# Spectral norms moved from the kernel's start into its first attention phase, in a two-layer attention kernel on one NeuronCore

## The chip, the core and the metric

The kernel runs on one NeuronCore of a Trainium2 chip. The metric is device time in microseconds (us), the median of several runs. Engines are named as in the profile: PE is TensorE's matrix multiply and PEld its weight load, DVE is VectorE, ACT is ScalarE, POOL is GpSimd, and SP is SyncE, which here only issues DMAs. ACTq and SPq are the issuing queues of ACT and SP.

## The reference, cut to what matters

Two layers run on x of shape (8, 64, 64, 256), in float32. The first layer is windowed attention over horizontal strips (half of the channels) and vertical strips (the other half), with a depthwise 3x3 convolution added. The second is attention over all 4096 positions of an image, with three small projections f, g and h and one out, v. The weights of these four are divided by their spectral norm, estimated with one power step:

```python
def _sn_kernel(w, u):
    wr = w.reshape(-1, w.shape[-1])
    v = _l2n(u @ wr.T)
    u2 = _l2n(v @ wr)
    sigma = v @ wr @ u2.T
    return w / sigma[0, 0]
...
qkv = x @ w_qkv + b_qkv                 # first layer
q, k = jnp.split(qkv, 2, axis=-1); v = k
context = jnp.concatenate([ch, cv], axis=-1)      # attention in strips
context = hard_swish(context + bias_branch)       # plus the convolution
x1 = context @ w_out + b_out
...
f = x1 @ kf + bf;  g = x1 @ kg + bg;  h = x1 @ kh + bh   # second layer
beta = softmax(g f^T)
out = gamma * ((beta h) @ kv + bv) + x1
```

The norms depend on weights alone. They are small: three weights of 256x32 and one of 32x256.

## The kernel before, in words

**Units and steps.** For each of the 8 images there are 8 horizontal units, 8 vertical units and 2 global units. A horizontal or vertical unit has 4 steps, a global one 32. A step computes a block of scores on PE (L696 or L877, four strips of 32 rows into two of three PSUM pairs), takes the exponential on ACT (L494, two pieces of 128x1024), and, one step later, multiplies the weights with the values (L713 or L893). Unit h0 takes the steps 0 to 3, h1 4 to 7, h2 8 to 11, h3 12 to 15, h4 16 to 19, and so on.

**What fills the steps.** Between scores and weighted sums PE does other work: the projections of x (L261, `project`: 32 matmuls of 128x256 for one group of 128 channels of one block of 512 positions), the sums of the weights (L731), later the projections of the second layer (L800, L827) and the outputs. ACT also evicts projections (L568 `qh`, L583 `kh`, L571, L586, L587), copies sums and results (L514 `copy_sums`, L743 `release`), and starts each convolution with its first tap (L635). DVE does the other eight taps of a convolution (L639), adds weights (L722, L904), and turns tiles (L504 to L507, L649).

**One bank.** Projections, sums, `norms`, `combined_weights` and some others all use one PSUM tile with the tag `mm` (L291). It has one buffer, so each of them waits until the last one's result was copied out of it.

**The planner.** The order of every engine's instructions is fixed when the program is built. `Flow` (L76) keeps a clock for each engine, worked out from the prices in L51 to L55. Each piece of extra work is a `Task` with a due step, a step from which it is ready, the tasks it needs, and a chain of (engine, price) pairs. `Flow.step` (L207) writes the scores, then work that is due, then the weighted sums of the step before, then in `fill_pe` (L147) more work for PE: of the tasks that may begin, the one whose bank is already open, or else the one that is due first; of two with the same due step, the one added first. A task with `bank=True` may begin only when the planner's clock has passed `bank_free`. Then `fill_act` and `fill_dve` (L193) give those engines tasks until their clocks have caught up with PE's. Whatever a task's function issues goes to the engines' queues at that point, in program order on each engine.

**`combined_weights`** (L448) multiplies the normed weights of f, g and h by `w_out` once, so that the second layer's projections can read the first layer's context. It is a task with ready 16 and due 24; it runs at 136.54 us.

**The start.** Ahead of the planner's steps, the program loads the weights. On SP: `w_qkv` (L303), `b_qkv` (L305) and four copies of `wv`, one for each quarter of the partitions (L323); then the planner's first load of x (`load`, L551). On ACT: `wfgh` in three pieces (L308), `u_r`, `uv_r` and `gam` (L316), `w_out` (L328), `dw` (L330), `dw_bias` (L332), `b_out` (L334), `bfgh` (L336) and `bv` (L338). Then come the norms: products and sums on DVE (L350 to L367), three groups of matmuls with ones on PE (L370, L371), a copy of the result out of `mm` (L375), DVE again (L378 to L388), one Sqrt on ACT (L389), and the scaling of the weights (L390 to L396). `w_out` and `dw` are multiplied by 1/6 (L397, L398). The temporary tiles lie in a pool, `prep`, that is closed at the end (L399), and its space is used again.

**The range of sums.** Each unit writes the reciprocals of its sums into `recs`, a tile of 128x18x16 per image. At an image's end `note` (L545) takes the elementwise maximum and minimum of `recs` and two tiles `seen`, also 128x18x16. After the last image `limits` (L411) reduces these to one value a row, compares them with bounds, and writes a flag; if a bound is passed, an exact but slower loop runs afterwards (L1334). It doesn't run here.

Of the kernel before, what the change touches and what calls it, by code (L numbers as in the profile page):

```python
# [23 lines left out]
D = 32  # L24
NQ = P // D
L2_EPS = 1e-12
# [4 lines left out]
def quad(r):  # L31
    return slice(r * D, (r + 1) * D)
# [20 lines left out]
ADD, NORM, SWISH, TAP, TAPS = 2.36, 2.5, 0.75, 0.75, 1.28  # L53
# [211 lines left out]
def tile_attention_blocks(  # L265
# [31 lines left out]
    ones = const.tile([P, P], F32, name="ones")  # L297
# [8 lines left out]
    raw = const.tile([P, 2, 3, D], F32, name="raw")  # L306
# [1 line left out]
        nc.scalar.dma_start(out=raw[:, :, z, :], in_=wfgh[z].rearrange("(k p) m -> p k m", p=P))  # L308


    prep_ctx = ExitStack()
    prep = prep_ctx.enter_context(tc.tile_pool(name="prep", bufs=1))

    def rows(ap, n, name):
        t = prep.tile([P, n], F32, name=name)
        nc.scalar.dma_start(out=t, in_=ap.to_broadcast([P, n]))  # L316
        return t

    u_r = rows(ufgh.rearrange("z o d -> o (z d)"), 3 * D, "u_r")

    wv_raw = prep.tile([P, C], F32, name="wv_raw")
    for r in range(NQ):
        nc.sync.dma_start(out=wv_raw[quad(r), :], in_=wv)  # L323
    uv_r = rows(uv, C, "uv_r")
    gam = rows(gamma, 1, "gam")

    wout_sb = const.tile([P, 2, C], F32, name="wout_sb")
    nc.scalar.dma_start(out=wout_sb, in_=w_out.rearrange("(k p) m -> p k m", p=P))  # L328
    dw_sb = const.tile([P, 2, 9], F32, name="dw_sb")
# [3 lines left out]
    bout_c = const.tile([P, 2], F32, name="bout_c")  # L333
# [3 lines left out]
    bv_c = prep.tile([P, 2], F32, name="bv_c")  # L337
    nc.scalar.dma_start(out=bv_c, in_=bv)  # L338

    wcomb = const.tile([P, 2, 3 * D], F32, name="wcomb")  # L340
    bcomb = const.tile([P, 2], F32, name="bcomb")
    wv_sb = const.tile([P, C], F32, name="wv_sb")
    bias_o = const.tile([P, 2], F32, name="bias_o")


    NF = 3 * D + 3
    flat = raw.rearrange("p k z d -> p k (z d)")
    ext = prep.tile([P, 2, NF], F32, name="ext")
    a_f = prep.tile([P, 2, 3], F32, name="a_f")
    nc.vector.tensor_mul(  # L350
        ext[:, :, : 3 * D], flat, u_r.unsqueeze(1).to_broadcast([P, 2, 3 * D])
    )
    nc.vector.tensor_reduce(
        a_f, ext[:, :, : 3 * D].rearrange("p k (z d) -> p k z d", d=D), AX.X, ALU.add
    )
    for k in range(2):
        nc.vector.tensor_mul(
            ext[:, k, : 3 * D].rearrange("p (z d) -> p z d", d=D), raw[:, k],
            a_f[:, k, :].unsqueeze(2).to_broadcast([P, 3, D]),
        )  # L360
    nc.vector.tensor_mul(ext[:, :, 3 * D :], a_f, a_f)
    ext_v = prep.tile([P, C + 1], F32, name="ext_v")
    a_v = prep.tile([P, 1], F32, name="a_v")
    nc.vector.tensor_mul(ext_v[:, :C], wv_raw, uv_r)
    nc.vector.tensor_reduce(a_v, ext_v[:, :C], AX.X, ALU.add)
    nc.vector.tensor_scalar_mul(ext_v[:, :C], wv_raw, a_v)
    nc.vector.tensor_mul(ext_v[:, C:], a_v, a_v)  # L367
    pb = mm_tile("norms")
    for k in range(2):
        nc.tensor.matmul(pb[:, :NF], lhsT=ones, rhs=ext[:, k, :], start=(k == 0), stop=(k == 1))  # L370
    nc.tensor.matmul(  # L371
        pb[:, NF : NF + C + 1], lhsT=ones[:D, :], rhs=ext_v[:D, :], start=True, stop=True
    )
    sums = prep.tile([P, NF + C + 1], F32, name="sums")
    nc.vector.tensor_copy(sums, pb[:, : NF + C + 1])  # L375

    a2, b2, inv = (prep.tile([P, 4], F32, name=n) for n in ("a2", "b2", "inv"))
    nc.vector.tensor_copy(a2[:, :3], sums[:, 3 * D : NF])  # L378
    nc.vector.tensor_copy(a2[:, 3:], sums[:, NF + C :])
    nc.vector.tensor_mul(sums, sums, sums)  # L380
    nc.vector.tensor_reduce(
        b2[:, :3], sums[:, : 3 * D].rearrange("p (z d) -> p z d", d=D), AX.X, ALU.add
    )
    nc.vector.tensor_reduce(b2[:, 3:], sums[:, NF : NF + C], AX.X, ALU.add)
    nc.vector.tensor_scalar_max(a2, a2, L2_EPS)
    nc.vector.reciprocal(a2, a2)
    nc.vector.tensor_mul(b2, b2, a2)
    nc.vector.tensor_scalar_max(inv, b2, L2_EPS)  # L388
    nc.scalar.activation(inv, inv, AF.Sqrt)  # L389
    nc.vector.reciprocal(b2, b2)  # L390
    nc.vector.tensor_mul(inv, inv, b2)
    for k in range(2):
        nc.vector.tensor_mul(raw[:, k], raw[:, k], inv[:, :3].unsqueeze(2).to_broadcast([P, 3, D]))

    nc.vector.tensor_scalar(wv_sb, wv_raw, inv[:, 3:], gam, ALU.mult, ALU.mult)
    nc.vector.scalar_tensor_tensor(bias_o, bv_c, gam, bout_c, ALU.mult, ALU.add)  # L396
    nc.vector.tensor_scalar_mul(wout_sb, wout_sb, 1.0 / 6.0)  # L397
    nc.vector.tensor_scalar_mul(dw_sb, dw_sb, 1.0 / 6.0)  # L398
    prep_ctx.close()  # L399


    seen = [const.tile([P, 2 * NB + 2, TB // D], F32, name=f"seen{i}") for i in range(2)]
    for t in seen:
        nc.gpsimd.memset(t, 1.0)

    check = ctx.enter_context(tc.tile_pool(name="check", bufs=1))
    lim = check.tile([P, 2], F32, name="lim")
# [14 lines left out]
    def attention(images, load_x, out_rows, exact):  # L422
# [113 lines left out]
        def image(b):  # L536
            hv, qh, kh, kn, xt, vs, part = {}, {}, {}, {}, {}, {}, {}

            @cache
            def recs():  # L540
                return work.tile(
                    [P, 2 * NB + 2, TB // D], F32, tag="recs", name=f"recs_{b}", bufs=out_bufs
                )

            def note():  # L545
                for t, op in zip(seen, (ALU.max, ALU.min)):
                    nc.vector.tensor_tensor(t, t, recs(), op)

            def load(i):
                xt[i] = xpool.tile([P, 2, TB], F32, tag="x", name=f"x_{b}_{i}")  # L550
# [297 lines left out]
            def global_unit(z):  # L848
# [149 lines left out]
        units, t = [], 0  # L998
# [118 lines left out]
        def inside_due(i, far):  # L1117

            n = i + min(i, INSIDE) + far
            return DUE["spread0"] + (DUE["spread1"] - DUE["spread0"]) * n // (NB + INSIDE)  # L1120

        for n, im in enumerate(ims):
# [4 lines left out]
            for i in range(NB):  # L1127
# [32 lines left out]
                for half in range(2):  # L1160
# [50 lines left out]
            for kind, k in (("f", 0), ("f", 1), ("h", 0), ("f", 2), ("f", 3), ("h", 1)):  # L1211
# [10 lines left out]
                else:  # L1222
# [9 lines left out]
                        bank=True,  # L1232
# [156 lines left out]
```

## Time and profile before

| what | value |
| --- | --- |
| time, median of 3 runs | 3414.65 us (3414.16 to 3418.29) |
| the profiled execution's own time | 3416.28 us |
| its span, first to last instruction | 3414.5 us |
| mean granted PE clock | 0.996 of full |
| PE, DVE, ACT, POOL busy | 3331.6, 2860.6, 2668.8, 63.5 us |
| first projection of x on PE | at 12.94 us |
| scores of step 0, step 8, step 16, step 24 | at 21.84, 59.07, 97.40, 135.47 us |

In lines of the order of time and of the groups, the columns are: start in us, length in us, engine, line of the code, operation, output<-input, shape, count, and in brackets the idle time of that engine just before and what ended it. In the view of waits, the columns are: who waited, for whom, us in total, times, and the longest. In the chain of waits: start, length, what. A busy time of PE is modelled, and neighbouring groups of matmuls overlap by a little.

Some durations of the start, which no other place of the kernel shows: DVE's first part of the norms takes 1.29 us (from L350 to the end of L361) and 1.33 us (L364 to the end of L367); the matmuls take 1.15 and 1.22 us; from the copy L375 to the end of L388 pass 2.45 us; Sqrt takes 0.21 us; the rest, L390 to L395, about 1.2 us. From issue to landing, `w_qkv` takes 4.2 us and the first block of x 4.5 us (each 512 KB); the median of all blocks of x is 3.7 us. The small loads take between 2.9 and 4.3 us.

### The profile page before, as it was taken

How to read it: one execution, taken by the hardware profiler on the slowest of the kernel's cores; microseconds unless marked ns; L12 is line 12 of the kernel's file. 1: busy time of each engine (PE TensorE's matmuls, PEld its weight loads, DVE VectorE, ACT ScalarE, POOL GpSimd, SP SyncE). 2: the span in 40 equal slices, each digit the busy share in tenths (PEclk: the TensorE clock that was granted, in tenths of full speed). 3: DMA queues.
4: the chain of work that ended last, by engine and by line, in shares of the span. 5: the costliest groups of instructions: out<-in, count | busy, mean ns of one | idle time of the engine just before them, and what ended most of it. 6: DMA issues, size and time to landing. Idle time of an engine off the chain costs nothing.

```text
span 3414.5 us, 78286 instructions
## 1 busy us (share of the span) xinstructions
PE 3331.6 (98%) x33780; PEld 1126.4 (33%) x33780; DVE 2860.6 (84%) x2340; ACT 2668.8 (78%) x3235; POOL 63.5 (2%) x266
## 2 busy tenths in 40 slices
PE   8989999999999999999999999999999999999998
PEld 3323333333333333333333333333333333333322
DVE  4778789887898879988799887998879988798886
ACT  5777787887778877788787887788877888778876
POOL 0000000000000000000000000000000000000000
PEclk9999999999999999999999999999999999999999
DMA  2122102221022210322112311123111231112200
GB/s 71 51 78 71 46 26 91 77 76 44 20 94 87 64 57 14 103 85 56 51 37 86 90 51 47 42 81 97 44 48 50 78 94 48 38 57 67 82 27 33
DMA packets 249410, 209.82 MB, mean 61 GB/s; under 512 B 26080, under 2 KB 190432, under 8 KB 249056
## 3 DMA queue, kind: packets, MB, share of 16 engines
q1 hardware_dynamic: 246816, 204.18, 19.7%
q8 instruction: 267, 4.37, 0.5%
q10 hardware_dynamic: 2240, 0.56, 0.1%
q14 instruction: 87, 0.71, 0.1%
HBM read 99.78 MB, written 83.89 MB: 54 GB/s over the span
## 4 chain that ended last, share of the span: by engine, by line
PE 71%; DVE 14%; ACT 8%; issue 4%; DMA 2%; SPq 1%; DVEq 0%; ACTq 0%
PE s L696 12%; PE s L877 11%; PE pq L261 11%; DVE acc_l L904 10%; PE num_l L893 10%; PE num_h L713 7%; PE s L261 6%; PE sum_h L731 5%; PE num_v L713 4%; ACT p_v L494 4%; PE sum_v L731 3%; DVE act L639 2%; PE pf L800 2%; ACT p_h L494 1%; PE s L932 1%
## 5 line engine op out<-in xcount | busy, mean ns | idle before, releaser
L904 DVE TENSOR_TENSOR acc_l<-acc_l,p_l 128x2048 f32<-128x2048 f32 x480 | 1099.8, 2291 | 224.5 <-ACT p_l L494 197.9
L494 ACT ACTIVATE p_l<-s 128x1024 f32<-128x1024 f32 x1024 | 992.6, 1025 | 187.5 <-PE s L877 120.7
L639 DVE SCALAR_TENSOR_TENSOR act<-hv,dw_sb,act 128x1024 f32<-128x1024 f32 x512 | 655.5, 1282 | 16.6 <-ACT act L635 2.3
L877 PE MATMUL s<-gq,f 32*128 32x512 f32 x4096 | 630.3, 640 | 4.3 <-ACT p_l L494 2.2
L494 ACT ACTIVATE p_h<-s 128x1024 f32<-128x1024 f32 x512 | 494.7, 1027 | 92.6 <-PE s L696 60.2
L494 ACT ACTIVATE p_v<-s 128x1024 f32<-128x1024 f32 x512 | 497.1, 1028 | 76.9 <-PE s L696 65.2
L893 PE MATMUL num_l<-p_l,h_sb 128*32 128x512 f32 x4096 | 545.5, 605 | 0.5 <-ACT nums_l L908 0.5
L261 PE MATMUL pq<-x,wqkv_sb 128*32 128x256 f32 x8192 | 521.3, 382 | 4.3 <-ACT qv L571 1.6
L261 PEld LDWEIGHTS pq<-x,wqkv_sb 128*32 128x32 f32 x8192 | 263.3, 111 | 362.1 <-issue 197.2
L696 PE MATMUL s<-qh,kh 32*128 32x512 f32 x2048 | 320.4, 641 | 11.4 <-ACT qh L568 6.6
L696 PE MATMUL s<-qv,kv 32*128 32x512 f32 x2048 | 327.1, 644 | 2.4 <-ACT p_v L494 2.4
L713 PE MATMUL num_v<-p_v,vs 128*32 128x512 f32 x2048 | 275.2, 609 | 21.7 <-DMA vs<-kvia 13.6
L877 PEld LDWEIGHTS s<-gq,f 32*128 32x128 f32 x4096 | 192.0, 182 | 312.1 <-issue 286.3
L713 PE MATMUL num_h<-p_h,vs 128*32 128x512 f32 x2048 | 271.9, 603 | 6.2 <-ACT nums_v L743 2.8
L261 PE MATMUL s<-act,wout_sb 128*32 128x512 f32 x2048 | 226.7, 594 | 0.0
L722 DVE TENSOR_TENSOR acc_v<-p_v,p_v 128x2048 f32<-128x2048 f32 x64 | 146.7, 2292 | 87.3 <-issue 60.6
L893 PEld LDWEIGHTS num_l<-p_l,h_sb 128*32 128x32 f32 x4096 | 80.7, 108 | 384.1 <-issue 371.3
L942 ACT ACTIVATE ot_l<-s,bias_o 128x512 f32<-128x512 f32 x120 | 76.3, 686 | 162.8 <-PE s L261 149.0
L722 DVE TENSOR_TENSOR acc_h<-p_h,p_h 128x2048 f32<-128x2048 f32 x64 | 146.4, 2288 | 33.9 <-PE sum_v L731 15.7
L696 PEld LDWEIGHTS s<-qv,kv 32*128 32x128 f32 x2048 | 106.9, 184 | 181.6 <-issue 172.3
L696 PEld LDWEIGHTS s<-qh,kh 32*128 32x128 f32 x2048 | 94.0, 183 | 180.9 <-issue 139.9
L722 DVE TENSOR_TENSOR acc_v<-acc_v,p_v 128x2048 f32<-128x2048 f32 x64 | 146.3, 2285 | 4.7 <-ACT p_v L494 4.7
(129 smaller groups left out, 2472.1 us busy)
## 6 DMA issues: line engine op xcount, KB each, us to landing
x<-in_xT SPq DMA_DIRECT2D x92, 512.0 KB, 3.7
kvia<-kt SPq DMA_DIRECT2D x128, 256.0 KB, 2.4
vs<-kvia SPq DMA_DIRECT2D x512, 64.0 KB, 2.1
out<-ot_l SPq DMA_DIRECT2D x128, 256.0 KB, 2.1
via_v<-nums_v SPq DMA_DIRECT2D x64, 256.0 KB, 2.0
shuf_v<-via_v SPq DMA_DIRECT2D x256, 64.0 KB, 2.1
f<-fg SPq DMA_DIRECT2D x256, 64.0 KB, 2.0
gq<-fg SPq DMA_DIRECT2D x64, 64.0 KB, 2.0
```

What stands on the lines that cost most here:

```text
L261: nc.tensor.matmul(out[quad(r), :], lhsT=lhsT[:, quad(r)], rhs=rhs, start=start, stop=stop)
L494: nc.scalar.activation(pt[:, 2 * z : 2 * z + 2, :], sc[z], AF.Exp, scale=scale)
L639: nc.vector.scalar_tensor_tensor(o, src, wt, o, ALU.mult, ALU.add)
L696: nc.tensor.matmul(row_of(sc, r), lhsT=k[quad(r), c * P : (c + 1) * P], rhs=q[quad(r), :], start=True, stop=not exact,)
L713: nc.tensor.matmul(u["num"][quad(r), :], lhsT=vs[kind, i][:, r, c, :], rhs=u[c][:, r, :], start=(c == 0), stop=(c == 3),)
L722: nc.vector.tensor_add(u["acc"], u["acc"] if c == 2 else u[0], u[c])
L731: nc.tensor.matmul(u["sum"][quad(r), cols], lhsT=ones[:, :D], rhs=pt[:, r, cols], start=(k == 0), stop=(k == len(of) - 1),)
L800: nc.tensor.matmul(pf[quad(r), cols], lhsT=wcomb[:, k, quad(r % 2)], rhs=act_of(2 * p + r // 2, k, cols), start=(k == 0), stop=(k == 1),)
L877: nc.tensor.matmul(row_of(sc, r), lhsT=f4[quad(r), c * P : (c + 1) * P], rhs=gq[quad(r), z, :], start=True, stop=not exact,)
L893: nc.tensor.matmul(u["num"][quad(r), :], lhsT=h_sb[:, c, :], rhs=u[c][:, r, :], start=(c == 0), stop=(c == 4 * NB - 1),)
L904: nc.vector.tensor_add(u["acc"], u["acc"], u[c])
L942: nc.scalar.activation(ot, po, AF.Identity, bias=bias_o[:, m : m + 1])
```

## The change

The norms are put into a function `norms()`, which becomes a task for PE with ready 8 and due 16, and `combined_weights` now needs it. The four copies of `wv` move from SP's queue to ACT's, behind `bv`, together with the loads of `uv` and `gamma`; so the first load of x stands directly behind `b_qkv` on SP. `uv` is loaded straight into `ext_v`, which saves a tile. The two multiplications by 1/6 stay outside the function. The pool `prep` is no longer closed. Instead of two tiles of 128x18x16, `seen` is one tile with a column for each image, and `note` reduces `recs` into that column.

```diff
-    prep_ctx = ExitStack()
-    prep = prep_ctx.enter_context(tc.tile_pool(name="prep", bufs=1))
+    prep = ctx.enter_context(tc.tile_pool(name="prep", bufs=1))
...
-    wv_raw = prep.tile([P, C], F32, name="wv_raw")
-    for r in range(NQ):
-        nc.sync.dma_start(out=wv_raw[quad(r), :], in_=wv)
-    uv_r = rows(uv, C, "uv_r")
-    gam = rows(gamma, 1, "gam")
...
     nc.scalar.dma_start(out=bv_c, in_=bv)
 
+    wv_raw = prep.tile([P, C], F32, name="wv_raw")
+    for r in range(NQ):
+        nc.scalar.dma_start(out=wv_raw[quad(r), :], in_=wv)
+    ext_v = prep.tile([P, C + 1], F32, name="ext_v")
+    nc.scalar.dma_start(out=ext_v[:, :C], in_=uv.to_broadcast([P, C]))
+    gam = rows(gamma, 1, "gam")
+    nc.vector.tensor_scalar_mul(wout_sb, wout_sb, 1.0 / 6.0)
+    nc.vector.tensor_scalar_mul(dw_sb, dw_sb, 1.0 / 6.0)
...
+    def norms():
+
...
-    nc.vector.tensor_mul(ext_v[:, :C], wv_raw, uv_r)
+        nc.vector.tensor_mul(ext_v[:, :C], ext_v[:, :C], wv_raw)
...
-    nc.vector.tensor_scalar_mul(wout_sb, wout_sb, 1.0 / 6.0)
-    nc.vector.tensor_scalar_mul(dw_sb, dw_sb, 1.0 / 6.0)
-    prep_ctx.close()
-
-
-    seen = [const.tile([P, 2 * NB + 2, TB // D], F32, name=f"seen{i}") for i in range(2)]
-    for t in seen:
-        nc.gpsimd.memset(t, 1.0)
+    seen = const.tile([P, 2, B], F32, name="seen")
...
-        nc.vector.tensor_reduce(lim[:, 0:1], seen[0], AX.XY, ALU.max)
-        nc.vector.tensor_reduce(lim[:, 1:2], seen[1], AX.XY, ALU.min)
+        nc.vector.tensor_reduce(lim[:, 0:1], seen[:, 0, :], AX.X, ALU.max)
+        nc.vector.tensor_reduce(lim[:, 1:2], seen[:, 1, :], AX.X, ALU.min)
...
             def note():
-                for t, op in zip(seen, (ALU.max, ALU.min)):
-                    nc.vector.tensor_tensor(t, t, recs(), op)
+                for i, op in enumerate((ALU.max, ALU.min)):
+                    nc.vector.tensor_reduce(seen[:, i, b : b + 1], recs(), AX.XY, op)
...
         if not exact:
+            spectral = flow.add("pe", [(norms, [("pe", 1.0), ("dve", 6.0)])], 16, ready=8, bank=True)
             combined.append(
-                flow.add("pe", [(combined_weights, [("pe", 5.0), ("dve", NORM)])], 24, ready=16, bank=True)
+                flow.add(
+                    "pe", [(combined_weights, [("pe", 5.0), ("dve", NORM)])], 24, [spectral],
+                    ready=16, bank=True,
+                )
             )
```

The body of `norms()` is otherwise the code of L346 to L396, indented.

More of the change, by code (lines that the diff above doesn't have):

```diff
@@ L343, in tile_attention_blocks @@
     bias_o = const.tile([P, 2], F32, name="bias_o")
-    NF = 3 * D + 3
     flat = raw.rearrange("p k z d -> p k (z d)")
[L348 to L356, printed above, removed]
+    def norms():
+        NF = 3 * D + 3
+        ext = prep.tile([P, 2, NF], F32, name="ext")
+        a_f = prep.tile([P, 2, 3], F32, name="a_f")
@@ L357, in tile_attention_blocks @@
         nc.vector.tensor_mul(
-            ext[:, k, : 3 * D].rearrange("p (z d) -> p z d", d=D), raw[:, k],
-            a_f[:, k, :].unsqueeze(2).to_broadcast([P, 3, D]),
-        )
-    nc.vector.tensor_mul(ext[:, :, 3 * D :], a_f, a_f)
-    ext_v = prep.tile([P, C + 1], F32, name="ext_v")
-    a_v = prep.tile([P, 1], F32, name="a_v")
-    nc.vector.tensor_mul(ext_v[:, :C], wv_raw, uv_r)
-    nc.vector.tensor_reduce(a_v, ext_v[:, :C], AX.X, ALU.add)
-    nc.vector.tensor_scalar_mul(ext_v[:, :C], wv_raw, a_v)
@@ L367, in tile_attention_blocks @@
[L367 to L396, printed above, removed]
-    nc.vector.tensor_scalar_mul(wout_sb, wout_sb, 1.0 / 6.0)
-    nc.vector.tensor_scalar_mul(dw_sb, dw_sb, 1.0 / 6.0)
@@ L399, in tile_attention_blocks @@
-    prep_ctx.close()
-    seen = [const.tile([P, 2 * NB + 2, TB // D], F32, name=f"seen{i}") for i in range(2)]
-    for t in seen:
-        nc.gpsimd.memset(t, 1.0)
+            ext[:, :, : 3 * D], flat, u_r.unsqueeze(1).to_broadcast([P, 2, 3 * D])
+        )
+        nc.vector.tensor_reduce(
+            a_f, ext[:, :, : 3 * D].rearrange("p k (z d) -> p k z d", d=D), AX.X, ALU.add
+        )
+        for k in range(2):
+            nc.vector.tensor_mul(
+                ext[:, k, : 3 * D].rearrange("p (z d) -> p z d", d=D), raw[:, k],
+                a_f[:, k, :].unsqueeze(2).to_broadcast([P, 3, D]),
+            )
@@ new lines, in norms @@
+        nc.vector.tensor_mul(ext[:, :, 3 * D :], a_f, a_f)
+        a_v = prep.tile([P, 1], F32, name="a_v")
+        nc.vector.tensor_mul(ext_v[:, :C], ext_v[:, :C], wv_raw)
+        nc.vector.tensor_reduce(a_v, ext_v[:, :C], AX.X, ALU.add)
+        nc.vector.tensor_scalar_mul(ext_v[:, :C], wv_raw, a_v)
+        nc.vector.tensor_mul(ext_v[:, C:], a_v, a_v)
+        pb = mm_tile("norms")
+        for k in range(2):
+            nc.tensor.matmul(pb[:, :NF], lhsT=ones, rhs=ext[:, k, :], start=(k == 0), stop=(k == 1))
@@ new lines, in norms @@
+        nc.tensor.matmul(
+            pb[:, NF : NF + C + 1], lhsT=ones[:D, :], rhs=ext_v[:D, :], start=True, stop=True
+        )
+        sums = prep.tile([P, NF + C + 1], F32, name="sums")
+        nc.vector.tensor_copy(sums, pb[:, : NF + C + 1])
+        a2, b2, inv = (prep.tile([P, 4], F32, name=n) for n in ("a2", "b2", "inv"))
+        nc.vector.tensor_copy(a2[:, :3], sums[:, 3 * D : NF])
+        nc.vector.tensor_copy(a2[:, 3:], sums[:, NF + C :])
+        nc.vector.tensor_mul(sums, sums, sums)
@@ new lines, in norms @@
+        nc.vector.tensor_reduce(
+            b2[:, :3], sums[:, : 3 * D].rearrange("p (z d) -> p z d", d=D), AX.X, ALU.add
+        )
+        nc.vector.tensor_reduce(b2[:, 3:], sums[:, NF : NF + C], AX.X, ALU.add)
+        nc.vector.tensor_scalar_max(a2, a2, L2_EPS)
+        nc.vector.reciprocal(a2, a2)
+        nc.vector.tensor_mul(b2, b2, a2)
+        nc.vector.tensor_scalar_max(inv, b2, L2_EPS)
+        nc.scalar.activation(inv, inv, AF.Sqrt)
+        nc.vector.reciprocal(b2, b2)
+        nc.vector.tensor_mul(inv, inv, b2)
@@ L406, in tile_attention_blocks @@
+        for k in range(2):
+            nc.vector.tensor_mul(raw[:, k], raw[:, k], inv[:, :3].unsqueeze(2).to_broadcast([P, 3, D]))
+        nc.vector.tensor_scalar(wv_sb, wv_raw, inv[:, 3:], gam, ALU.mult, ALU.mult)
+        nc.vector.scalar_tensor_tensor(bias_o, bv_c, gam, bout_c, ALU.mult, ALU.add)
+    seen = const.tile([P, 2, B], F32, name="seen")
     check = ctx.enter_context(tc.tile_pool(name="check", bufs=1))
@@ L991, in attention @@
         if not exact:
+            spectral = flow.add("pe", [(norms, [("pe", 1.0), ("dve", 6.0)])], 16, ready=8, bank=True)
             combined.append(
-                flow.add("pe", [(combined_weights, [("pe", 5.0), ("dve", NORM)])], 24, ready=16, bank=True)
+                flow.add(
+                    "pe", [(combined_weights, [("pe", 5.0), ("dve", NORM)])], 24, [spectral],
+                    ready=16, bank=True,
+                )
             )
```

## The prediction, made before the changed kernel was run

> **What bounds the kernel now.** I read the page's first and fourth parts first, for the bound, and then the ends and the step the change touches.
>
> ```profile
> PE 3331.6 (98%) x33780; PEld 1126.4 (33%) x33780; DVE 2860.6 (84%) x2340; ACT 2668.8 (78%) x3235; POOL 63.5 (2%) x266
> ...
> PE 71%; DVE 14%; ACT 8%; issue 4%; DMA 2%; SPq 1%; DVEq 0%; ACTq 0%
> ```
>
> TensorE holds the chain almost everywhere, so a stall of PE is paid in full and a microsecond taken off the start is kept in full, because everything behind it moves along. Next I read the chain of waits up to 22 us (start, length, what).
>
> ```profile
> 5.56 3.43 DMA wout_sb<-in_w_out
> ...
> 9.01 3.03 DMA bv_c<-in_bv
> ...
> 12.37 0.53 DVE sums L375
> ...
> 12.94 3.69 PE pq L261 x32
> ...
> 16.65 0.70 ACT qh L568
> ```
>
> The first projection starts at 12.94. Ahead of it lies no useful work of PE, but the norms: small loads, VectorE, and the copy of the norms' sums (L375), which frees the one PSUM bank `mm`. The block of x was only just earlier. The waits of the DMA queue (first 12 us) and the order of time show why.
>
> ```profile
> SPq L323 <- DMA wqkv_sb<-in_w_qkv: 2.8, 1, 2.8
> ...
> SPq L551 <- DMA uv_r<-in_uv: 0.3, 1, 0.3
> ```
>
> ```profile
> 7.04 0.40 SPq L551 DMA_DIRECT2D x<-in_xT  x1
> ...
> 9.01 0.36 ACTq L338 DMA_DIRECT2D bv_c<-in_bv  x1
> ...
> 9.40 1.28 ACT L389 ACT_TABLE_LOAD   x1 [9.40 <-DMA dwb_sb<-in_dw_bias]
> ...
> 21.80 1.28 ACT L494 ACT_TABLE_LOAD   x1
> ```
>
> x is issued at 7.04 and takes 4.5 us to land: 11.5. It stands behind four `wv` issues on SP, whose second waits for `w_qkv` to land and x itself for `uv` (L551), though no data joins them. Three SP and five ACT transfers were under way when both queues stopped (2.8 to 5.0 us), so I read eight completion counters used in turn: a ninth transfer waits for the first. The whole ACT queue issues DMAs until 9.37; only then its first table load runs.
>
> The norms will go to step 16 of the first horizontal phase (below). The order of time there:
>
> ```profile
> 96.80 5.25 DVE L639 SCALAR_TENSOR_TENSOR act<-hv,dw_sb,act 128x1024 f32<-128x1024 f32 x4 [2.26 <-ACT act L635]
> ...
> 98.47 1.06 PE L713 MATMUL num_h<-p_h,vs 128*32 128x512 f32 x8
> ...
> 100.40 0.59 ACT L743 COPY nums_h<-num_h 128x512 f32<-128x512 f32 x1
> ...
> 102.19 0.59 ACT L514 COPY sum_sb_h<-sum_h 128x512 f32<-128x512 f32 x1 [1.20 <-PE sum_h L731]
> ...
> 103.12 1.93 PE L261 MATMUL pq<-x,wqkv_sb 128*32 128x256 f32 x32
> 103.30 1.93 ACT L494 ACTIVATE p_h<-s 128x1024 f32<-128x1024 f32 x2
> ```
>
> DVE idles 2.26 us ahead of four convolution taps, and ACT 1.20 us ahead of the sums' copy; PE has no gap between 97.40 and 106.9.
>
> **What the Trainium skill says.** "ScalarE: Activation LUTs", section "What ACT_TABLE_LOAD costs": a load takes about 1283 ns, with a drain of about 1380 on top. The trace agrees on the load (1.28 both times); the drain isn't visible as busy time. The same page, "Table sets": exp and sqrt lie in different sets, plain functions are in all. The trace agrees: one load ahead of Sqrt, one ahead of the first exp, none at identity or relu. "TensorE: Matmul & The Clock Gate", Part 1: after an idle window of some 3.4 us PE runs at half rate until about 3.4 us of work have passed. The trace fits: 32 projection matmuls take 3.64 us at 12.94 and 1.91 from 30 us on. "Trainium Kernel Development and Optimization", Key Constraints: queues of different engines share the same 16 DMA engines, so moving `wv` from SP to ACT saves only SP's issue time. No view here shows that apart.
>
> **The change, part by part.**
>
> *Start.* SP now issues w_qkv (0.74), b_qkv (1.25) and x at about 1.74, where `wv` stood; at most eight transfers are under way by then, so no counter holds it. w_qkv landed at 0.74 + 4.2 = 4.94. x has as many bytes (512 KB) behind it; the transfer view shows 316 and 380 GB/s in the busiest slices, thus 1.4 to 1.7 us more: x lands at about 6.5 (bounds: 1.74 + 3.7, the median of x, = 5.4; and 8 if the loads of ACT share the engines evenly). The projection takes 3.64 at the cold clock, to 10.2. But `qh` needs ACT, and ACT's queue grows from 12 to 16 issues. Counting eight counters in turn with landings of 3.3 to 4.2 us: the second round begins at 5.0, the last (`gamma`) waits for `b_out`, issued near 6.0 and landing 3.6 later, so ACT is done near 9.9. The first table load (1.28) then gives `qh` at 11.2 instead of 16.65: a gain of 5.4. Bounds: 6.5 if x alone limits (16.65 − 10.15); 3.4 if x still waits for w_qkv to land (5.0 + 4.5 + 3.7 = 13.2). The second table load at 21.80 goes, at no gain: PE's scores of 21.84 to 23.93 covered it. The freed `prep` pool's waits (14.3 us on POOL ahead of the `hv` memsets) go too; those tiles are first read by ACT at 25.78, so nothing.
>
> *Where norms runs.* Ready at 8, due at 16, it needs the bank. Each of the steps 8 to 15 holds one projection in that bank (the trace shows one per step), with dues of 8, 9, 9, 11, 12, 13, 13 and 15, all earlier. At 16 it ties with the row sums of h3 and comes first, having been added first. So PE gets it behind the weighted sums (98.47 to 99.5), ahead of the sums at 99.35; ACT gets Sqrt behind the copy L743; DVE gets its part ahead of the four taps, because the planner places the first tap in step 16's fill of DVE, which follows PE's.
>
> *Its price there*, in times of before. DVE's first part, L350 to L367, took 1.29 + 1.33 = 2.62 us; it begins at 94.5 in the gap and ends near 97.2, before PE arrives. That cover is worth up to 5 us, see the rivals. Matmuls: 1.15 + 1.22 cold; about 1.3 warm (an estimate, by 379 to 634 ns). Then the sums must wait for the copy L375: 0.6. PE: 99.5 + 1.9 = 101.4. ACT: exp to 100.5, copy to 101.1, table load to 102.4; VectorE's steps from L375 to L388 took 2.45, so `inv` is there at 103.3, Sqrt ends 103.55, the load back 104.85. The exp of step 17 starts then and not at 103.30; the copy of the sums is behind it (two pieces of the sums are left to step 17 by the planner), ending near 107.4; the next projection starts at 107.45 instead of 103.12, with the weighted sums moved ahead of it, and the scores of step 18 at 109.2 instead of 105.84. **Cost 3.4.** Bounds: 1.3 (matmuls alone, all of ACT's waiting absorbed; a gain is excluded, as PE gets more to do in a stretch without gaps) and 10.4 (below). DVE's rest, some 3.6 us, pushes taps back; DVE is idle for over 8 us between 102 and 140 and takes it up. SP and POOL get nothing from norms; no DMA moves with it. Behind it wait `combined_weights`, at 136.54, far later, and nothing else.
>
> *Range of sums.* Per image two operations of 450 ns become two reductions of 128x288, which L413 and L414 price at 447 and 443: nothing. The last two reductions shrink from 0.82 together to perhaps 0.35, but the end is paced by output tiles (ACT waits for `out` to land before four of the last six evictions): nothing. Two memsets on POOL (0.61) go, unseen. The scaling of `wout` and `dw` stays in the start, long before use.
>
> *Sum.* −5.4 + 3.4 = −2.0. The profiled execution took 3416.28 (span 3414.5 and 1.8 around it), 1.6 above the median of the runs. It would go to 3414.3, the median from 3414.65 to **3412.6**. About 0.2%, or 6.8 us, is what a measurement of this kernel tells from no change.
>
> **Rivals.** *Norms hidden and ACT early*: the table loads fall into gaps (ACT is busy only 78%) and x alone limits: −6.5 + 1.3 = −5.2, 3409.5. For: 1.20 us of idle ACT there. Against: two loads are 2.56 and exp is next.
> *The change doesn't do what it says*: x is still held by a counter, or ACT's 16 issues last longer; gain 3.4, net 0, 3414.7. For: the waits named at L323 and L551.
> *Slower: norms behind DVE's backlog.* If the planner emits the taps first, DVE reaches norms at 102.05 and its first part ends at 104.65. PE idles from 99.5, 5.15 us, past the 3.4 us of the clock gate; cold matmuls to 107.0, `inv` 109.5, Sqrt and load 111.0: exp 7.7 late, and some 2.7 for the half rate and the queue, 10.4. In addition the planner books 6 us of DVE and bank, so two steps may lose their projection, 1.9 each. −5.4 + 10.4 + 3.8 = +8.8: 3423.5. It decides when DVE starts norms later than about 97. For: combined_weights cost such a hole at 136. Against: the 2.26 us gap lies just where it is needed.
>
> **How the numbers follow.** Forecast 0.57 (its own range 3409.5 to 3416), hidden 0.17, start not gained 0.15, backlog 0.11. Later steps may be reordered by shifted planner clocks, and the cold start may end one window earlier or later, each some 2 us either way; so half of the hidden case and a little of the forecast pass 3407.8: faster 0.12. Backlog gives slower 0.10. Same 0.78. Range 3407.0 to 3419.0.
>
> **What would show it.** Right: x issued near 1.7, first projection near 6.5, `qh` near 11; norms' matmuls between weighted sums and row sums near 94, two more table loads around them, exp of the next step late by 1 to 3 us. Wrong: `qh` above 13 or below 10; PE idle over 3.4 us at norms with matmuls at 634 ns after it; spans of later images that differ from before by more than 2 us.

## The result, and the profile after

The changed kernel takes 3423.27 us (median of 20 runs, 3420.38 to 3425.41); the kernel before, run beside it, 3415.44 (20 runs, 3411.90 to 3419.17). The ratio is 1.0023, 95% interval 1.0017 to 1.0029: 7.8 us slower, where 2.0 us faster was forecast. The time lies above the range (3407 to 3419).

The page of the changed kernel, in the parts that were read of the one before (its busy times, its chain by engine). One group of its list of costly instructions is added: busy time and mean ns, then idle time of PE ahead of it.

```profile
PE 3332.7 (97%) x33780; PEld 1124.4 (33%) x33780; DVE 2860.1 (84%) x2340; ACT 2666.6 (78%) x3236; POOL 62.3 (2%) x264
...
PE 72%; DVE 15%; ACT 7%; issue 3%; DMA 1%; SPq 1%; ACTq 0%; DVEq 0%
...
L711 PE MATMUL num_v<-p_v,vs 128*32 128x512 f32 x2048 | 277.4, 614 | 29.0 <-DMA vs<-kvia 19.8
```

The same group on the page of the kernel before:

```profile
L713 PE MATMUL num_v<-p_v,vs 128*32 128x512 f32 x2048 | 275.2, 609 | 21.7 <-DMA vs<-kvia 13.6
```

PE does the same 33780 matmuls in 1.1 us more, and the span grew by 7.2. PE's idle time ahead of the weighted sums of vertical units is 7.3 us longer, 6.2 of it in waits for `vs`, the turned values. That is tempting as the answer, but 6.0 of the 6.2 lie between 180 and 430 us (13.8 against 7.8), that is in image 0, where the kernel as a whole loses 2.4 (steps 32 to 128 of the table below). Totals can't say where the time goes. (Line numbers behind the edit are two lower than before: the weighted sums L713 are now L711.)

The start went as forecast. This is its order of time:

```profile
1.74 0.44 SPq L549 DMA_DIRECT2D x<-in_xT  x1
6.90 3.64 PE L261 MATMUL pq<-x,wqkv_sb 128*32 128x256 f32 x32 [6.90 <-DMA x<-in_xT]
10.21 0.44 ACTq L315 DMA_DIRECT2D gam<-in_gamma  x1
10.69 1.28 ACT L566 ACT_TABLE_LOAD   x1 [10.69 <-DMA wv_raw<-in_wv]
11.98 0.69 ACT L566 ACTIVATE qh<-pq,bqkv_sb 128x512 f32<-128x512 f32 x1
```

x is issued at 1.74 and lands at 6.90; `qh` comes at 11.98 instead of 16.65, and it waits for ACT's queue, not for PE. Norms stands where it was expected too:

```profile
94.28 0.69 PE L373 MATMUL norms<-ext,ones 128*128 128x99 f32 x4
94.90 0.69 PE L374 MATMUL norms<-ext_v,ones 32*128 32x257 f32 x2
95.82 1.28 ACT L392 ACT_TABLE_LOAD   x1
96.22 1.07 PE L729 MATMUL sum_h<-p_h,ones 128*32 128x256 f32 x16 [0.62 <-DVE sums L378]
98.32 0.20 ACT L392 ACTIVATE inv<-inv 128x4 f32<-128x4 f32 x1 [1.22 <-DVE inv L391]
98.54 1.28 ACT L492 ACT_TABLE_LOAD   x1
99.84 1.94 ACT L492 ACTIVATE p_h<-s 128x1024 f32<-128x1024 f32 x2
...
101.01 1.14 PE L694 MATMUL s<-qh,kh 32*128 32x512 f32 x8
...
102.31 1.93 PE L261 MATMUL pq<-x,wqkv_sb 128*32 128x256 f32 x32 [0.16 <-ACT sum_sb_h L512]
```

The products start without a wait, the sums wait 0.62 for the copy, and there are two table loads. The scores of step 18 (101.01) stand ahead of the next projection (102.31). Nothing here is 10 us long. To find the loss I took the start of every step's scores from the trace, and subtracted that of the kernel before. A number that stays the same from step to step is a delay that is only carried along; where it changes, time is lost or won. (One execution each; the columns to the right are the experiments below.)

| step | what it is | changed | no booking | empty booking | due 14 | due 20 | two swaps | norms at step 4 |
|---|---|---|---|---|---|---|---|---|
| 4 | image 0, h1 | −5.17 | −3.15 | −0.23 | −4.54 | −4.73 | −6.01 | −4.21 |
| 16 | h4; norms | −5.18 | −3.16 | −0.24 | −3.07 | −4.74 | −6.02 | −1.84 |
| 32 | v0 | −1.58 | +1.83 | −0.54 | −2.93 | −3.33 | −2.42 | −0.16 |
| 128 | image 0, l1 | +0.79 | +2.75 | +0.68 | +12.95 | +16.95 | −1.73 | −0.78 |
| 172 | image 1, v3 | +1.52 | +2.37 | +1.41 | +12.55 | +16.55 | −1.02 | −1.17 |
| 190 | image 1, v7 | +11.23 | +2.21 | +11.12 | +12.12 | +16.14 | −1.24 | −1.36 |
| 1023 | last | +8.55 | −1.46 | +11.49 | +11.42 | +15.49 | −1.08 | −3.94 |

The gain of 5.2 at the start is kept up to step 16, and 3.6 of it is gone by step 32. Then 9.7 us are lost in eighteen steps of image 1's vertical units, half a millisecond behind anything that the change touched. That stretch, one row from the table of windows for each kernel: length, busy time of each engine (instructions), granted clock of PE, DMA share, GB/s. First the changed kernel, then the one before.

```profile
654.90:718.00 63.10, 57.91 (x516) 17.95 (x512) 44.32 (x47) 46.18 (x55) 0.00 (x0) 0.92 0.30 85
```

```profile
653.40:706.80 53.40, 51.74 (x516) 17.80 (x512) 44.89 (x49) 45.69 (x55) 0.00 (x0) 1.00 0.36 103
```

The same 516 matmuls keep PE busy for 57.91 us instead of 51.74, 6.2 us more. The clock of 0.92 instead of 1.00 accounts for about 5 of them (0.08 × 63.1); the last 1 us isn't explained. The idle time, 63.1 − 57.9 = 5.2 against 1.7, is 3.5 longer. Together 9.7.

What PE waits for there is seen in the order of time. The changed kernel around step 172:

```profile
651.30 0.71 DVE L502 STREAM_TRANSPOSE zt_v<-sum_sb_v 128x512 f32<-128x512 f32 x1
...
653.09 0.69 DVE L746 TENSOR_TENSOR nums_v<-nums_v,sum_sb_v 128x512 f32<-128x512 f32 x1
...
653.69 2.28 DVE L720 TENSOR_TENSOR acc_v<-p_v,p_v 128x2048 f32<-128x2048 f32 x1
...
654.92 1.13 PE L694 MATMUL s<-qv,kv 32*128 32x512 f32 x4
...
656.09 3.77 ACT L492 ACTIVATE p_v<-s 128x1024 f32<-128x1024 f32 x4 [1.76 <-PE s L694]
...
657.17 1.13 PE L694 MATMUL s<-qv,kv 32*128 32x512 f32 x4 [1.13 <-ACT p_v L492]
...
659.45 2.09 PE L694 MATMUL s<-qv,kv 32*128 32x512 f32 x8
```

And one unit of the kernel before, for the same three kinds of work:

```profile
660.02 2.29 DVE L722 TENSOR_TENSOR acc_v<-p_v,p_v 128x2048 f32<-128x2048 f32 x1 [2.12 <-issue]
...
661.06 1.94 ACT L494 ACTIVATE p_v<-s 128x1024 f32<-128x1024 f32 x2 [0.51 <-PE s L696]
661.89 1.37 PE L696 MATMUL s<-qv,kv 32*128 32x512 f32 x8
662.23 0.71 DVE L504 STREAM_TRANSPOSE zt_v<-sum_sb_v 128x512 f32<-128x512 f32 x1
```

Before, DVE first adds two of a unit's four weight tiles (`acc_v<-p_v,p_v`) and then normalizes the unit before (from `zt_v` on). In the changed kernel the two are the other way round. There are three buffers of weights, so the exponential of a unit's fourth step takes the buffer of its first, which the addition reads: it can't start until the addition has ended, at 653.69 + 2.28 = 655.97, and ACT starts at 656.09. The view names PE as the releaser, since the newest scores ended at 656.05; but ACT's first exponential needs the scores of the step before, done at 653.99. PE then waits 1.13 for ACT, and the next scores take 2.09 instead of 1.37. The same comes once more at 670. The windows of the changed kernel, 3.4 us each, show how each wait is followed by a slow stretch; there is a third pair at 700:

```profile
655.50:658.90 3.40, 2.27 (x16) 0.46 (x12) 3.40 (x4) 2.81 (x4) 0.00 (x0) 1.00 0.00 0
658.90:662.30 3.40, 3.40 (x16) 0.72 (x16) 1.68 (x3) 2.17 (x4) 0.00 (x0) 0.51 0.47 128
...
669.20:672.60 3.40, 2.26 (x12) 0.52 (x14) 3.40 (x3) 2.44 (x3) 0.00 (x0) 1.00 0.30 93
672.60:676.00 3.40, 3.40 (x20) 0.57 (x16) 0.87 (x2) 1.92 (x3) 0.00 (x0) 0.50 0.18 50
...
699.90:703.30 3.40, 0.87 (x8) 0.04 (x4) 2.81 (x5) 2.39 (x3) 0.00 (x0) 1.00 0.63 169
703.30:706.70 3.40, 3.16 (x16) 0.75 (x16) 2.36 (x2) 0.00 (x0) 0.00 (x0) 0.50 0.78 224
```

The third wait is another one: PE waits 2.77 us for `vs`, a DMA, where the kernel before waits 1.3. So the two swapped pairs directly account for two of the three slow stretches. Each stretch of 3.4 us at half rate costs 1.7, and the three together the 5 us of clock.

Why does DVE's order differ in image 1? Norms is a task of the planner, which takes the bank `mm` at step 16. The row sums of h3 then go to step 17, all clocks of the planner shift against each other, and the list that it writes differs from the one before in 146 of the steps 16 to 205; from 206 on it is the same. Worked out with VectorE prices of 0.5, 1, 2.5 and 8 instead of 6.0, the planner's list is the same; it isn't the 6.0 that matters.

**Theory:** the order in steps 16 to 205 makes the loss, and the swapped pairs of addition and normalization, with what the planner puts behind them, most of it. **Rivals:** norms' own stall with its table loads; the buffers of `prep`, kept to the end.

### The profile page after: what moved, and what is told of

Read it like the earlier page. It is cut to its first block, busy times and chain, and to the rows that moved or that the text cites. A ratio compares the mean times of both kernels' runs of the same rounds, so it can differ in the third digit from the quotient of the medians.

```text
span 3421.7 us, 78247 instructions
## 1 busy us (share of the span) xinstructions
PE 3332.7 (97%) x33780; PEld 1124.4 (33%) x33780; DVE 2860.1 (84%) x2340; ACT 2666.6 (78%) x3236; POOL 62.3 (2%) x264
## 4 chain that ended last, share of the span: by engine, by line
PE 72%; DVE 15%; ACT 7%; issue 3%; DMA 1%; SPq 1%; ACTq 0%; DVEq 0%
PE s L694 12%; PE s L875 11%; PE pq L261 10%; PE num_l L891 10%; DVE acc_l L902 9%; PE num_h L711 6%; PE s L261 6%; PE num_v L711 5%; PE sum_h L729 5%; ACT p_v L492 3%; PE sum_v L729 3%; DVE act L637 3%; PE pf L798 2%; ACT p_h L492 1%; PE s L930 1%
## 5 line engine op out<-in xcount | busy, mean ns | idle before, releaser
L492 ACT ACTIVATE p_l<-s 128x1024 f32<-128x1024 f32 x1024 | 991.5, 1023 | 188.9 <-PE s L875 118.9
L711 PE MATMUL num_v<-p_v,vs 128*32 128x512 f32 x2048 | 277.4, 614 | 29.0 <-DMA vs<-kvia 19.8
L711 PE MATMUL num_h<-p_h,vs 128*32 128x512 f32 x2048 | 271.9, 603 | 6.2 <-ACT nums_v L741 2.7
L720 DVE TENSOR_TENSOR acc_h<-p_h,p_h 128x2048 f32<-128x2048 f32 x64 | 146.4, 2288 | 36.0 <-PE sum_v L729 14.1
```

Source lines behind the costliest of these rows:

```text
L492: nc.scalar.activation(pt[:, 2 * z : 2 * z + 2, :], sc[z], AF.Exp, scale=scale)
L711: nc.tensor.matmul(u["num"][quad(r), :], lhsT=vs[kind, i][:, r, c, :], rhs=u[c][:, r, :], start=(c == 0), stop=(c == 3),)
L720: nc.vector.tensor_add(u["acc"], u["acc"] if c == 2 else u[0], u[c])
```

## The experiments

Each ran 5 to 21 times beside the kernel before, on one of three chips. `[…]` is the 95% interval of the ratio.

| run | median us | before, same chip | ratio |
|---|---|---|---|
| no booking | 3412.53 | 3416.25 | 0.9990 [0.9982, 0.9999] |
| empty booking | 3425.66 | 3416.25 | 1.0027 [1.0017, 1.0037] |
| due 14 | 3425.78 | 3416.25 | 1.0030 [1.0018, 1.0042] |
| due 20 | 3433.68 | 3416.25 | 1.0052 [1.0038, 1.0065] |
| two swaps | 3416.30 | 3415.68 | 1.0004 [0.9995, 1.0012] |
| two swaps, no square root | 3414.51 | 3415.68 | 0.9997 [0.9989, 1.0006] |
| start only | 3416.35 | 3415.68 | 1.0006 [0.9998, 1.0014] |
| range only | 3415.67 | 3415.68 | 0.9999 [0.9990, 1.0007] |
| norms at step 4 | 3408.22 | 3416.28 | 0.9979 [0.9972, 0.9987] |
| norms at step 4, late loads | 3410.51 | 3416.28 | 0.9985 [0.9979, 0.9992] |

**No booking.** Against the changed kernel:

```diff
                 def release():
...
                     nc.scalar.copy(u["num_sb"], u["num"])
+                    if nm == "0_h3" and not exact:
+                        norms()
...
-            spectral = flow.add("pe", [(norms, [("pe", 1.0), ("dve", 6.0)])], 16, ready=8, bank=True)
...
-                    "pe", [(combined_weights, [("pe", 5.0), ("dve", NORM)])], 24, [spectral],
+                    "pe", [(combined_weights, [("pe", 5.0), ("dve", NORM)])], 24,
```

> The changed kernel, but norms() is no task of the planner: it is called behind the eviction of the weighted sums of horizontal unit 3, the place where the changed kernel issues it, and the planner's clocks know nothing of it, so all other work stands in the order of the kernel before. Theory (the booking shifts the planner's clocks and the order written from them in steps 16 to 205 loses some 12 us): 3410 to 3413 us, 2 to 5 us under the kernel before, and the start of step 188 some 3 to 5 us earlier than before instead of 12.5 later. Rival (norms itself, its two table loads or the buffers it holds cost the time): 3421 to 3425 us, as the changed kernel.

Measured 3412.53, ratio 0.9990: inside the theory's range. The whole of the move is in it, at the same place, and the loss of steps 172 to 190 is not (+2.37, then +2.21). But the expected 3 to 5 us ahead at step 188 weren't there (it is 2.4 behind). This one trace gets ahead only later in the run, by what isn't shown, so the median fits the theory in part by luck. Here norms costs 5.0 us in steps 16 to 22, more than in the changed kernel: 2.1 by step 18, with PE's products and the wait for the copy, and 2.9 by step 22. The order of time of that second part:

```profile
98.23 1.07 PE L729 MATMUL sum_h<-p_h,ones 128*32 128x256 f32 x16 [0.62 <-DVE sums L378]
...
101.62 5.24 DVE L637 SCALAR_TENSOR_TENSOR act<-hv,dw_sb,act 128x1024 f32<-128x1024 f32 x4
...
110.38 2.25 DVE L720 TENSOR_TENSOR acc_h<-p_h,p_h 128x2048 f32<-128x2048 f32 x1
...
112.72 1.94 ACT L492 ACTIVATE p_h<-s 128x1024 f32<-128x1024 f32 x2 [2.16 <-DVE acc_h L720]
...
115.87 0.42 PE L261 MATMUL pq<-x,wqkv_sb 128*32 128x256 f32 x4 [3.10 <-ACT kv L585]
```

DVE gets to its four taps at 101.62, after norms' 4.1 us; ten microseconds later ACT waits 2.16 for the next addition, and PE 3.10 for ACT. That VectorE's extra work makes this addition late is read from the order; the run at step 4 below tests it.

**Empty booking.** Against the kernel before, whose norms stay in the start:

```diff
+            spectral = flow.add(
+                "pe", [(lambda: None, [("pe", 1.0), ("dve", 6.0)])], 16, ready=8, bank=True
+            )
...
-                flow.add("pe", [(combined_weights, [("pe", 5.0), ("dve", NORM)])], 24, ready=16, bank=True)
+                flow.add(
+                    "pe", [(combined_weights, [("pe", 5.0), ("dve", NORM)])], 24, [spectral],
+                    ready=16, bank=True,
+                )
```

> The kernel before, norms left in the start, with an empty task in the planner at the same place and price (1.0 of TensorE, 6.0 of VectorE, the bank), which the combined weights wait for. It issues no instruction; only the order of the rest is that of the changed kernel. Theory (order): 3425 to 3430 us, 10 to 14 us over the kernel before, most of it between steps 172 and 190. Rival (norms itself, its table loads or buffers): 3415 us, as the kernel before.

Measured 3425.66: 9.4 us slower without one instruction changed, only their order. From step 46 to step 256 its scores start within 0.23 us of the changed kernel's, and the row of windows is the same to 0.02 us of busy PE:

```profile
654.80:717.90 63.10, 57.89 (x516) 17.96 (x512) 44.32 (x47) 46.19 (x55) 0.00 (x0) 0.92 0.29 85
```

With the run without booking this rules both rivals out as the cause of that loss. It also prices norms in the order of the changed kernel: from step 16 to 32 that kernel loses 3.6 and this one wins 0.3, so norms costs 3.9. Of these, 2.1 are there at step 18, 3.2 at step 22, and all from step 24 on.

**Due 14, due 20.** Only the 16 in the task is changed, to 14 or 20.

> The changed kernel with the norms task due at step 14 instead of 16, at the same price. The order then differs from that of the kernel before in steps 14 to 112 only; from step 113 on it is the same. Theory (the order in image 1's vertical phase loses some 10 us): that loss is gone, steps 172 to 190 add nothing, 3411 to 3417 us depending on what the other order of image 0 costs. Rival (norms itself): 3421 to 3425 us.

> The changed kernel with the norms task due at step 20 instead of 16, at the same price. The order differs from that of the kernel before in steps 20 to 112 only. Theory (the order in image 1's vertical phase loses some 10 us): steps 172 to 190 add nothing, 3411 to 3417 us. Rival (norms itself): 3421 to 3425 us.

The mechanism held and the time did not. Steps 172 to 190 add nothing (+12.55 to +12.12, +16.55 to +16.14), as expected. But 3425.78 and 3433.68 are not 3411 to 3417: these two lose 16 and 20 us between steps 32 and 128, in image 0, where the changed kernel loses 2.4. I had taken image 1 for the sore place. It isn't one: each list differs from the one before in other steps, and each loses, at a place of its own. In the run due at 20, PE waited 16.5 us for `vs` in image 0's vertical units and the start of its global ones (180 to 430 us):

```profile
PE num_v L711 <- DMA vs<-kvia: 16.5, 4, 6.0
PE s L694 <- ACT p_v L492: 3.0, 5, 1.1
PE s L875 <- DMA gq<-fg: 2.3, 1, 2.3
```

But in the same stretch the run due at 14 waited 14.1 for `vs`, the changed kernel 13.8 and the kernel before 7.8. So this wait alone doesn't tell the two slow lists from the changed kernel's.

**Two swaps.** Against the changed kernel, with its booking. The rule names units 0 to 2; the planner's list shows that unit 0 had the order of before already, so two pairs change.

```diff
+                u.pair = acc
...
+        for u, nxt in zip(units, units[1:]):
+            if u.kind == nxt.kind == "v" and 160 <= u.t < 172 and not exact:
+                u.normed.after.append(nxt.pair)
```

> The changed kernel with its booking as it is, and one rule more for the planner: the normalizations of vertical units 1 and 2 of image 1 may run only after the first addition of exponentials of the next unit. That puts these two pairs of VectorE tasks back into the order of the kernel before, and the planner then writes the same order as there from step 174 on. Theory (in the changed kernel the addition stands behind the normalization, so its weights' buffers come free late, ScalarE's exponentials wait for it, TensorE waits for those, and the clock is halved after that): the 10 us of steps 172 to 190 are gone, 3411 to 3414 us. Rival (the loss there comes from the work done before, in image 0, and would show whatever the two pairs do): 3421 to 3424 us.

The loss of steps 172 to 190 is gone, in full:

```profile
652.40:705.70 53.30, 51.85 (x520) 17.92 (x520) 45.69 (x51) 45.63 (x56) 0.00 (x0) 1.00 0.36 103
```

The clock is 1.00 again, all three slow stretches are gone, and step 190 stands at −1.24 instead of +11.23. The median, 3416.30, is 7.0 us under the changed kernel's, and 2.3 over the upper end expected. So two pairs of tasks that changed places, and what the planner put behind them because of that, are the larger part of the loss. What is left is hardly a gain: of the 6.0 us ahead at step 16, 1.2 are left at step 190.

**Two swaps, no square root.** `AF.Sqrt` becomes `AF.Identity`.

> As the run with the two pairs put back, but ScalarE's square root in norms() is an identity, so it loads no table (the output's scale of two weights is then wrong; the instructions and their sizes are otherwise the same). It prices the two table loads in the middle of the horizontal phase. Theory of the prediction (they delay the exponentials of step 17 and what waits for them by some 3 us): 2 to 3 us under the run with the two pairs put back. Rival (the buffers of the next exponentials and later waits swallow it): within 1 us of that run.

In the traces the rival holds: from step 16 to 32 this run loses 3.58, the run with the square root 3.60. The medians don't decide it: they are 1.8 us apart, between the two forecasts, and their intervals overlap. With the square root, both table loads lie in the stretch. Without them the exponential of step 17 starts 4.97 us after norms' first product, in the changed kernel 5.56, and the scores of step 18 start 6.7 us after it in both.

**Start only.** The kernel before, with the loads of `wv`, `uv` and `gamma` moved behind the others on ACT, and norms left in the start.

> The kernel before with one part of the change alone: the loads of wv, uv and gamma go behind the others on ScalarE's queue, so that x is issued directly behind the weights on SP, and the norms stay in the start. Theory (TensorE takes the norms' products ahead of the first projection, and those now wait for wv, issued last): x lands at 6.5 us but the first projection starts at 13 to 16 us, and the time is 3414 to 3419 us. Rival (the earlier x alone brings the 5 us): 3409 to 3411 us.

3416.35, in the theory's range. The order of time shows what the early x meets:

```profile
1.74 0.44 SPq L552 DMA_DIRECT2D x<-in_xT  x1
...
14.24 1.22 PE L372 MATMUL norms<-ext_v,ones 32*128 32x257 f32 x2 [4.42 <-DVE ext_v L368]
16.08 3.64 PE L261 MATMUL pq<-x,wqkv_sb 128*32 128x256 f32 x32 [0.62 <-DVE sums L376]
```

The projection starts at 16.08, later than before (12.94). The early load is worth something only with norms out of its way. In this trace the scores are 5.6 us late at step 4, yet only 0.8 at the last step. So in a single trace a loss at the start needn't reach the end; what takes it back isn't shown.

**Range only.** The kernel before with `seen`, `note` and `limits` of the changed one.

> The kernel before with one part of the change alone: the range of the sums is kept per image by two reductions, instead of by two comparisons into tables of 288 numbers each. Both theories: the same time as the kernel before within 1 us, as VectorE has slack where they stand. A time 2 us or more under or over it would mean that this part had been misjudged.

3415.67 against 3415.68. This part costs and gains nothing.

**Norms at step 4.** The run without booking, with `"0_h0"` for `"0_h3"`.

> As the run without booking, so in the order of the kernel before, but norms() is called behind the eviction of horizontal unit 0 (step 4) instead of unit 3 (step 16). There VectorE is busy only 4.1 of 10.2 us in the kernel before, and ScalarE 6.7; at step 16 to 20 VectorE is busy 10.0 of 11.0. Theory (the 5 us that norms cost at step 16 to 20 without booking come from its VectorE work and table loads delaying taps and the next addition, where VectorE has no slack): the cost falls to the products of TensorE and a short wait, 2 to 3 us, and the time is 3409 to 3412 us. Rival (the cost goes with norms wherever it stands): 3412 to 3414 us, as without booking.

Measured 3408.22, 8.1 us under the kernel before; 0.8 us under the lower end expected. The cost is 2.4 (−4.21 at step 4, −1.83 at step 8). Another 1.7 goes at step 16, where this execution has half rate from 97.1 to 100.5 us; the next run, with norms at the same place, has full rate there and loses nothing. At step 190 the trace is 1.4 ahead and at the last step 3.9, so the greater part of the 8.1 lies in no step that was explained. Against the run without booking (3.7 under the kernel before) the intervals still overlap a little. Its order of time:

```profile
40.82 0.69 PE L373 MATMUL norms<-ext,ones 128*128 128x99 f32 x4
...
41.56 1.28 ACT L392 ACT_TABLE_LOAD   x1
...
42.76 1.93 PE L261 MATMUL pq<-x,wqkv_sb 128*32 128x256 f32 x32 [0.62 <-DVE sums L378]
...
46.42 1.28 ACT L492 ACT_TABLE_LOAD   x1
...
47.71 1.94 ACT L492 ACTIVATE p_h<-s 128x1024 f32<-128x1024 f32 x2
```

PE pays its two products and the 0.62 for the copy; DVE had the room. (The 10.0 of 11.0 in the expectation are steps 18 and 19; in 16 and 17 VectorE was busy 6.8 of 8.4 us.) ACT had more room too, so the two aren't told apart here. The table loads are in the same order as at step 16.

**Norms at step 4, late loads.** The same, and what nothing reads before norms is loaded on SP behind x; `w_out` is multiplied by 1/6 in `norms()`:

```diff
...
                 nc.sync.dma_start(out=xt[i], in_=load_x(b, i))
+                if not exact and b == 0 and i == 0:
+                    late_loads()
```

> As the run with norms at step 4, and what only norms and the combined weights read (ufgh, wv, uv, w_out, four small vectors) is loaded on SP's queue behind the first block of x, so that ScalarE's queue has 5 transfers to issue at the start instead of 17, and its first table load and first eviction are not behind them (in the changed kernel they start at 10.7 and 12.0 us, while the first projection ends at 10.5). Theory: the first eviction starts 1 to 1.5 us earlier, and so does all that follows, 3408 to 3411 us. Rival (the first second of scores waits for something else, or the loads slow x): no difference from the run with norms at step 4.

`qh` comes 1.7 us earlier (10.34 against 12.05), but the median isn't under that of the run before it, and the intervals overlap. What comes next was late instead:

```profile
10.34 0.69 ACT L571 ACTIVATE qh<-pq,bqkv_sb 128x512 f32<-128x512 f32 x1 [3.48 <-PE pq L261]
...
22.05 1.93 PE L716 MATMUL num_h<-p_h,vs 128*32 128x512 f32 x8 [4.15 <-DMA vs<-kvia]
```

The scores of step 0 start 3.4 us earlier than in the run before it, and PE gives most of that back: it waits 4.15 for the first values, and its clock is at half rate from 20.1 to 26.9; at step 4 the two are 0.5 apart.

## Why the prediction was wrong, by its own steps

- **Start, −5.4:** right in its steps, and in size for this trace: −5.2 at step 4; x at 6.90 (6.5 forecast), ACT's queue done at 10.65 (9.9), `qh` at 11.98 (11.2). That ACT, and not x, sets `qh` was right. But −5.2 is one draw. Six more traces have the same start, and their gain at step 4 is between 1.5 and 6.0 (mean of the seven 4.2): the run with −6.0 has full rate from 11.2 on, the one with −1.5 (no square root) half rate from 23.2 to 30.0. The width that the text gave the cold start, some 2 us either way, is the size of it.
- **Where norms runs:** right in each point: step 16, behind the weighted sums, ahead of the row sums, the first part on DVE hidden (it ran from 89.3 to 91.8).
- **Its price there, +3.4:** the size is near, 3.9 (and 5.0 without booking), but by chance, as the reason failed. The chain held as far as the projection: in times of before (5.18 added), the exponential of step 17 starts at 105.0 (104.85 forecast) and the projection at 107.5 (107.45). But the scores of step 18 don't wait for it. They stand ahead of it, at 106.2 and not 109.2, only 0.3 later than before. The forecast charged it to the two table loads by way of that exponential; without them the price was the same up to step 32. On ACT the Trainium skill ("ScalarE: Activation LUTs", "What ACT_TABLE_LOAD costs") adds a drain to each load. Here the exponential started 0.02 us after the load's end (98.54 + 1.28, then 99.84). In the run without booking 2.9 of the 5.0 come where ACT waits for DVE, where I wrote "DVE is idle for over 8 us between 102 and 140 and takes it up". What makes the 1.8 of the 3.9 that come after step 18 isn't shown.
- **Range of sums, 0:** right (ratio 0.9999).
- **The step that failed:** "Later steps may be reordered by shifted planner clocks … each some 2 us either way". It was in the text as a width, not as a term of the sum. Measured by the empty booking it is +9.4 us in the median, and +11.5 at the last step of its trace, of which 9.7 are steps 172 to 190. Three other lists gave +9.5 (due 14), +17.4 (due 20), and, with the two swaps, +0.6, each with the gain of the start and the price of norms in it. "Either way" was wrong as well, for the lists tried: none with a booking came out ahead by more than its interval. With the terms as measured, −5.2 + 3.9 + 9.4 = +8.1, beside the 7.8 of the result (+9.1 with the mean start).
- **Rival "norms behind DVE's backlog", 3423.5:** the time is right by chance. It needed DVE to start norms after 97, and DVE had ended the first part at 91.8. Its tail, "two steps may lose their projection", named the booking, but as lost work of PE at step 16; and the price of 6 us that it blamed plays no part.
- **What would show it wrong:** "spans of later images that differ from before by more than 2 us" was the sign that came.
- The clock's share was left out of it too. I had half rate only for a wait beyond 3.4 us, after the two states that the Trainium skill lists ("TensorE: Matmul & The Clock Gate", Part 1). Two of the windows above were followed by half rate with PE busy 2.27 and 2.26 of 3.40 us and no single wait over 1.14. The measurement decides: here a third of a window idle was enough. It isn't a rule, though: in the same trace PE is busy 1.74 of 3.40 us from 170.8 to 174.2, and full rate follows. What decides it, these runs don't settle.

Open: why image 0's vertical units are so costly in the lists of due 14 and due 20; why the third wait at 700, for `vs`, is longer; and the slow drift of −2 to −4 us between step 190 and the end in some of the runs against the one trace of the kernel before.

## What to carry to other kernels

Where a planner writes a static order, a task that is moved or booked changes every decision behind it, so compare the written order of all engines first, and find the first step and the last at which they differ. Then price the move with the order held still, and the order with no move; together the two experiments tell order from work. Don't take a gain at the start from one trace: here the same start gave 1.5 to 6.0 us. Look for a place by the slack of the engines that carry the work (here at step 4), not by where its result is due.

## What was not expected of the hardware

- The half-rate stretches behind waits of 1.13 and 1.14 us, and one behind 2.77: of the 9.7 us lost in steps 172 to 190, about 5 are clock and 3.5 are waiting.
- An activation table that is loaded twice (2 × 1.28 us) in a stretch where TensorE sets the end cost nothing that the two traces show (3.58 against 3.60 with them, up to step 32).
